# Slabs of two 64-slot units in a GRU with a top-2 mixture of experts, on one core

## The chip, the cores and the metric

One Trainium2 chip, one of its cores. The metric is device time in microseconds, the median of several executions. The engines are named as in the profile: PE (TensorE matmul), PEld (TensorE weight load), DVE (VectorE), ACT (ScalarE), POOL (GpSimd), SP (SyncE, which here issues nearly all DMAs). All data are float32.

## The reference

A GRU runs over `x` of shape (16, 256, 512): 16 sequences, 256 time steps, state size 512, started from `cond_2048`. Each of its 4096 output tokens then goes through a mixture of 8 experts, and the result is added to `x`.

```python
gi = x @ W_ih + b_ih;  gh = h @ W_hh + b_hh        # per time step
r = sigmoid(i_r + h_r); z = sigmoid(i_z + h_z)
n = tanh(i_n + r * h_n)
h_new = (1.0 - z) * n + z * h
...
router_logits = x / norm @ router_w                # x: the GRU's outputs, 4096 x 512
routing_weights = softmax(router_logits)
rw, selected_experts = top_k(routing_weights, 2);  rw = rw / sum(rw)
combine = sum(one_hot(selected_experts, 8) * rw[..., None], axis=1)
for e in range(8):
    out = out + combine[:, e, None] * (x @ Wa[e] @ Wb[e])   # Wa 512x128, Wb 128x512
...
x = x + out
```

## The kernel before

**The recurrence.** `step` (L910) emits one time step. The state lies as 128 partitions by 128 (four groups of 32, of which 16 rows are sequences), so that all matmuls use 32 columns of PE and four of them, one for each column group, run beside each other. PE multiplies the state with W_hh into the banks `rn` (L921) and `z` (L931). ACT forms `r` (L947) and `z` (L952), DVE `n` in two instructions (L954, L955), ACT its tanh (L956), and DVE `zh`, `m` and the new state `rows` (L959, L961, L963), which it transposes for PE (`hist`, L966). The next step's first matmul waits for that transpose. The part of W_ih (L269, L277) of the pair of steps to come is spread over the two steps before. Eight steps are a block of 128 tokens.

**The mixture.** Blocks 0 to 28 are dispatched, in four chunks of 7, 11, 7 and 4 blocks (`CHUNKS`). `Route` (L592) finds a block's two experts; its instructions on POOL are `nrm` (L629), a memset (L307) and `pre` (L637). When a chunk is complete, `Chunk` (L436) ranks its tokens, gives each expert a run of slots whose length is rounded up to 128, and POOL scatters the rows into slots in DRAM (L558, two indirect DMAs for each block). `Slab` (L648) then works on 128 slots of one expert. It loads the slots (`xg`, four DMAs of SP). POOL reads the expert's number into a register (L672) and copies the expert's Wa and Wb into `wag` and `wbg` (L677, L681). DVE transposes (`xgT`, L687). PE multiplies with Wa (L698; two halves, `down`) and with Wb (L713; two halves, `up`), ACT empties PSUM, and SP stores to DRAM. `Combine` (L737) gathers a block's two rows of each token back (L750, two indirect DMAs of POOL), and DVE adds them to `x` (L764). Blocks 29 to 31 are not dispatched: `Moe` (L778) runs all eight experts on them (L833, L854, L870).

A chunk of k blocks gets `(2 * 128 * k + 127 * 8) // 128` slabs, whatever the routing: 21, 29, 21 and 15, together 86.

**What sets the order.** All instructions are emitted in one order, and `keep_order` holds every engine to it. A planner places the mixture's work among the steps. Each agent's `plan` is a list of `Piece`s with a `gap` (steps since the piece before), a `cost` of PE time, and the buffers it `takes` and `gives` (counted in `ROOM`, L29). In each step `choose` (L1052) goes through the agents in order of rank; a piece with a cost is taken while the step's spare time (0.5, and 1.8 in the steps named by `EARLY`) is not used up, or against a credit that grows with the work left and the time to its deadline (L1060, L1073). After step 256 there is no recurrence left, and the rounds follow each other without it. A slab's plan before:

```python
Piece(then=[("load",)], takes="xg load", gives="load"),
Piece(gap=2, then=[("weights",)], takes="wg copy", gives="copy"),
Piece(gap=2, then=[("turn",)], takes="xt turn", gives="xg turn"),
Piece(cost=0.43, pe=[("down", 0)], takes="ps"),
Piece(gap=0, cost=0.43, pe=[("down", 1)], then=[("mid",)], takes="at", gives="ps xt"),
Piece(cost=0.43, pe=[("up", 0)], takes="ps"),
Piece(gap=0, cost=0.43, pe=[("up", 1)], then=[("store",)], gives="ps wg at"),
```

There are four buffers for the weights of slabs, so the copies for slab n+4 wait for the matmuls of slab n. The 12 `EARLY` pairs of steps had their W_ih part done long before, so their steps have 1.3 us of PE work less.

Of the kernel before, what the change touches and what calls it, by code (L numbers as in the profile page):

```python
# [8 lines left out]
FP = mybir.dt.float32  # L9
I32 = mybir.dt.int32  # L10
# [11 lines left out]
P = 128  # L22
TS = 8
CHUNKS = [7, 11, 7, 4]
LAG = 10
# [4 lines left out]
    "ps": 3, "xg": 4, "wg": 4, "xt": 2, "at": 2, "yg": 2, "xr": 3, "a": 1, "aT": 1,  # L30
    "hc": 1, "load": 2, "copy": 1, "turn": 2, "early": 2,
# [13 lines left out]
def gru_moe_kernel(  # L45
# [55 lines left out]
    HE = E // 2  # L101

# [43 lines left out]
    for side, src in enumerate((b_ih, b_hh)):  # L146
        for g in (0, 2, 1):
            tag = ("xg", "wbg")[side]
            b_rows[side, g] = slb.tile([1, D], FP, tag=tag, name=f"b_{side}_{g}")
            act.dma_start(b_rows[side, g], src[None, g * D : (g + 1) * D])  # L150
# [31 lines left out]
    SM = max((2 * P * k + (P - 1) * E) // P for k in CHUNKS)  # L182
    pages = const.tile([P, KM], FP, name="pages")
    for k in range(KM):
        pool.memset(pages[:, k : k + 1], float(P * k))
    count = const.tile([P, SM], FP, name="count")
    for k in range(SM):
        pool.memset(count[:, k : k + 1], float(k))
    before = const.tile([P, E, E], FP, name="before")
    pool.memset(before, 0.0)  # L190
    for e in range(1, E):
# [6 lines left out]
    n_slots = [  # L198
        max((2 * P * k + (P - 1) * E) // P for k in CHUNKS[n::2]) for n in range(2)
    ]  # L200
# [235 lines left out]
    class Chunk:  # L436


        def __init__(self, c, k):
            self.c, self.k = c, k  # L440
            self.n_slabs = (2 * P * k + (P - 1) * E) // P
# [30 lines left out]
        def places(self):  # L472
            c, k, S = self.c, self.k, self.n_slabs
            full = chk.tile([P, E, KM], FP, tag="full", name=f"full_{c}")
            dve.tensor_tensor(
                full[:, :, 0:k],
                self.rank[:, k, :, None].broadcast_to([P, E, k]),
                pages[:, None, 0:k].broadcast_to([P, E, k]),
                ALU.is_gt,
            )  # L480
            t8 = chk.tile([P, E], FP, tag="t8", name=f"t8_{c}")
            dve.reduce_sum(t8, full[:, :, 0:k], axis=AX.X)
            self.t8 = t8

        def places2(self):
# [10 lines left out]
                sv, first[:, None, :].broadcast_to([P, k, E]), float(P),  # L496
# [22 lines left out]
        def experts(self):  # L519
            c, k, S = self.c, self.k, self.n_slabs  # L520
            end = chk.tile([P, E], FP, tag="end", name=f"end_{c}")
            dve.tensor_add(end, self.first, self.t8)
            past = chk.tile([P, SM, E - 1], FP, tag="past", name=f"past_{c}")
# [6 lines left out]
            ef = chk.tile([P, SM], FP, tag="ef", name=f"ef_{c}")  # L530
            dve.reduce_sum(ef[:, 0:S], past[:, 0:S, :], axis=AX.X)
            self.expert = chk.tile([P, SM], I32, tag="expert", name=f"expert_{c}")
# [115 lines left out]
    class Slab:  # L648
# [21 lines left out]
        def weights(self):  # L670
            n = self.n
            e = pool.value_load(  # L672
                self.chunk.expert[0:1, n : n + 1], min_val=0, max_val=E - 1
            )
            self.wa = slb.tile([P, NQ, R], FP, tag="wag", name=f"wag_{self.name}")
            self.wb = slb.tile([P, D], FP, tag="wbg", name=f"wbg_{self.name}")
            pool.tensor_copy(  # L677
                self.wa,
                wa_sb[:, :, bass.ds(e, 1), :].rearrange("p q e r -> p (q e) r"),
            )  # L680
            pool.tensor_copy(  # L681
                self.wb, wb_sb[:, bass.ds(e, 1), :].rearrange("p e f -> p (e f)")
            )
# [8 lines left out]
        def down(self, n):  # L692
            if n == 0:
                self.ps = big(f"at_ps_{self.name}")
            for q in (2 * n, 2 * n + 1):
                for c in range(NJ):
                    c32 = slice(32 * c, 32 * c + 32)
                    pe.matmul(  # L698
                        self.ps[c32, 0:P], lhsT=self.wa[:, q, c32],
                        rhs=self.xt[:, q, :], start=(q == 0), stop=(q == NQ - 1),  # L700
# [6 lines left out]
        def up(self, n):  # L707
# [3 lines left out]
            for c in range(NJ):  # L711
                c32 = slice(32 * c, 32 * c + 32)
                pe.matmul(  # L713
                    self.ps[c32, half], lhsT=self.at[:, c32], rhs=self.wb[:, half],
# [9 lines left out]
        def plan(self):  # L724
            return [
                Piece(then=[("load",)], takes="xg load", gives="load"),
                Piece(gap=2, then=[("weights",)], takes="wg copy", gives="copy"),
                Piece(gap=2, then=[("turn",)], takes="xt turn", gives="xg turn"),
                Piece(cost=0.43, pe=[("down", 0)], takes="ps"),
                Piece(gap=0, cost=0.43, pe=[("down", 1)], then=[("mid",)],  # L730
                      takes="at", gives="ps xt"),
                Piece(cost=0.43, pe=[("up", 0)], takes="ps"),
                Piece(gap=0, cost=0.43, pe=[("up", 1)], then=[("store",)],
                      gives="ps wg at"),
# [43 lines left out]
    class Moe:  # L778
# [4 lines left out]
        def prep(self):  # L783
# [7 lines left out]
            self.sq = moe.tile([P, NQ, P], FP, tag="a", bufs=1, name=f"sq_{i}")  # L791
# [28 lines left out]
        def soft3(self):  # L820
# [4 lines left out]
            self.a = moe.tile([P, E, R], FP, tag="a", bufs=1, name=f"a_{i}")  # L825
            self.aT = moe.tile([P, E, P], FP, tag="aT", bufs=1, name=f"aT_{i}")
# [16 lines left out]
        def scale(self, s):  # L843
            e4 = slice(s * HE, (s + 1) * HE)
            dve.tensor_mul(
                self.a[:, e4, :],
# [4 lines left out]
        def trans(self, s):  # L851
            ps = big(f"aT_ps_{self.i}_{s}")
            for k in range(HE):
                pe.transpose(  # L854
                    ps[:, k * P : (k + 1) * P], self.a[:, s * HE + k, :], ident
                )
            self.ps["t", s] = ps

        def evict(self, s):
            act.copy(  # L860
                self.aT[:, s * HE : (s + 1) * HE, :].rearrange("p e t -> p (e t)"),
# [3 lines left out]
        def up(self, e):  # L865
            if e == 0:
                self.ps["o"] = big(f"o_ps_{self.i}")
            for c in range(NJ):
# [3 lines left out]
                    lhsT=self.aT[:, e, c32],  # L872
# [138 lines left out]
    n_slabs = [(2 * P * k + (P - 1) * E) // P for k in CHUNKS]  # L1011
# [186 lines left out]
```

## Time and profile before

| | |
|---|---|
| time, median of 6 executions | 1302.6 us (1300.65 to 1305.58) |
| the profiled execution's own time | 1303.33 us |
| its span, first to last instruction | 1301.6 us |
| busy PE / PEld / DVE / ACT / POOL | 1254.1 / 896.0 / 737.7 / 391.3 / 285.4 us |
| mean granted PE clock | 0.99 |
| POOL copies `wag` (L677) | 86, 661 ns mean |
| POOL copies `wbg` (L681) | 86, 649 ns mean |
| first `hist` transpose ends (step 1) | 36.7 us |
| last `hist` transpose ends (step 256) | 1219.2 us |

How to read it: "busy" is the time in which an engine has an instruction under way, and a line such as "L677 POOL COPY wag<-wa_sb 128x512 f32 x86" is a group of 86 instructions of line 677 which write `wag` from `wa_sb`. In a timeline the columns are the start and the duration in us, engine, line, operation, output and input, shape and count; in brackets, the idle time of the engine ahead of it and what ended that. A matmul of float32 shows as two instructions, each with its own weight load.

The time falls into three parts: 36.7 us until the first step is done, 1182.5 us for the other 255 steps, and 82.4 us after the last one.

### The profile page before, as it was taken

How to read it: one execution, taken by the hardware profiler on the slowest of the kernel's cores; microseconds unless marked ns; L12 is line 12 of the kernel's file. 1: busy time of each engine (PE TensorE's matmuls, PEld its weight loads, DVE VectorE, ACT ScalarE, POOL GpSimd, SP SyncE). 2: the span in 40 equal slices, each digit the busy share in tenths (PEclk: the TensorE clock that was granted, in tenths of full speed). 3: DMA queues.
4: the chain of work that ended last, by engine and by line, in shares of the span. 5: the costliest groups of instructions: out<-in, count | busy, mean ns of one | idle time of the engine just before them, and what ended most of it. 6: DMA issues, size and time to landing. Idle time of an engine off the chain costs nothing. (4 is left out here: it accounts for less than half of the span.)

```text
span 1301.6 us, 68450 instructions
## 1 busy us (share of the span) xinstructions
PE 1254.1 (96%) x30378; PEld 896.0 (69%) x30378; DVE 737.7 (57%) x2678; ACT 391.3 (30%) x1354; POOL 285.4 (22%) x504
## 2 busy tenths in 40 slices
PE   7899999999999999999999989999999999999986
PEld 3577777777677777777776756777777778777642
DVE  1455555556565555555656636666566466776643
ACT  1232222222232333333333323333333323333220
POOL 2000000002321100000102313232114234273542
PEclk7999999999999999999999989999999999999999
DMA  8532322222422212111112644654336456674786
GB/s 209 146 128 70 134 79 84 99 67 82 154 79 67 61 49 55 57 47 56 56 44 76 194 142 117 177 154 142 97 95 204 134 151 172 192 229 141 214 243 179
DMA packets 149477, 158.67 MB, mean 122 GB/s; under 512 B 22646, under 2 KB 103606, under 8 KB 149180
## 3 DMA queue, kind: packets, MB, share of 16 engines
q1 hardware_dynamic: 139760, 123.83, 32.3%
q0 software_dynamic: 9280, 30.42, 7.6%
q8 instruction: 238, 3.90, 1.3%
q14 instruction: 59, 0.48, 0.1%
q10 hardware_dynamic: 140, 0.05, 0.0%
HBM read 84.21 MB, written 69.99 MB: 118 GB/s over the span
## 5 line engine op out<-in xcount | busy, mean ns | idle before, releaser
L921 PE MATMUL rn<-whh,hist 128*32 128x256 f32 x8160 | 495.4, 382 | 16.9 <-DVE hist L966 14.0
L921 PEld LDWEIGHTS rn<-whh,hist 128*32 128x32 f32 x8160 | 251.1, 110 | 196.5 <-DVE hist L966 48.8
L269 PE MATMUL rn<-wih,xT 128*32 128x256 f32 x3712 | 291.5, 383 | 13.6 <-DMA wih<-in_L_cond_W_ih_dram 7.9
L954 DVE SCALAR_TENSOR_TENSOR n<-r,rn 128x128 f32<-128x128 f32 x256 | 73.4, 287 | 367.9 <-ACT r L947 367.7
L931 PE MATMUL z<-whh,hist 128*32 128x128 f32 x8160 | 272.5, 273 | 0.0
L931 PEld LDWEIGHTS z<-whh,hist 128*32 128x32 f32 x8160 | 236.6, 110 | 41.9 <-issue 0.2
L947 ACT ACTIVATE r<-rn 128x128 f32<-128x128 f32 x256 | 71.1, 278 | 427.6 <-PE rn L921 426.7
L277 PE MATMUL z<-wih,xT 128*32 128x128 f32 x3712 | 192.5, 275 | 0.0
L277 PEld LDWEIGHTS z<-wih,xT 128*32 128x32 f32 x3712 | 124.6, 111 | 79.3 <-issue 2.7
L269 PEld LDWEIGHTS rn<-wih,xT 128*32 128x32 f32 x3712 | 115.3, 111 | 15.5 <-ACT rn L249 6.3
L952 ACT ACTIVATE z<-z 128x128 f32<-128x128 f32 x256 | 71.1, 278 | 150.5 <-PE z L931 150.5
L959 DVE SCALAR_TENSOR_TENSOR zh<-z,h 128x128 f32<-128x128 f32 x255 | 77.8, 305 | 65.3 <-ACT z L952 64.7
L629 POOL TENSOR_TENSOR nrm<-ss,half 128x1 f32<-128x1 f32 x29 | 16.3, 561 | 405.9 <-ACT ht L627 385.9
L698 PE MATMUL at_ps<-xgT,wag 128*32 128x128 f32 x2752 | 98.6, 274 | 3.3 <-POOL nrm L815 1.7
L713 PE MATMUL y_ps<-wbg,at 128*32 128x256 f32 x1376 | 96.2, 380 | 0.1
L698 PEld LDWEIGHTS at_ps<-xgT,wag 128*32 128x32 f32 x2752 | 81.0, 111 | 10.1 <-issue 3.5
L966 DVE STREAM_TRANSPOSE hist<-rows 128x128 f32<-128x128 f32 x256 | 79.8, 312 | 8.7
L974 DVE STREAM_TRANSPOSE h<-hist 128x128 f32<-128x128 f32 x256 | 79.7, 311 | 8.7
L963 DVE SCALAR_TENSOR_TENSOR rows<-zh,m 128x128 f32<-128x128 f32 x256 | 76.9, 301 | 8.9
L681 POOL COPY wbg<-wb_sb 128x512 f32 x86 | 55.8, 649 | 115.3 <-PE y_ps L713 115.3
L721 ACT COPY y<-y_ps 128x512 f32<-128x512 f32 x86 | 50.2, 584 | 97.6 <-PE y_ps L713 86.0
L956 ACT ACTIVATE n<-n 128x128 f32<-128x128 f32 x256 | 77.2, 302 | 4.8 <-DVE n L955 4.5
(136 smaller groups left out, 1056.3 us busy)
## 6 DMA issues: line engine op xcount, KB each, us to landing
xg<-x_slots SPq DMA_DIRECT2D x344, 64.0 KB
y_slots<-y SPq DMA_DIRECT2D x86, 256.0 KB
ht<-H SPq DMA_DIRECT2D x58, 256.0 KB
x_slots<-zero SPq DMA_DIRECT2D x50, 256.0 KB
x<-in_x_dram SPq DMA_DIRECT2D x256, 32.0 KB
xr<-in_x_dram SPq DMA_DIRECT2D x32, 256.0 KB
out_dram<-xr SPq DMA_DIRECT2D x32, 256.0 KB
H<-rows SPq DMA_DIRECT2D x232, 32.0 KB
```

The lines of the kernel that those rows point to most:

```text
L269: pe.matmul(rn[32 * j : 32 * j + 32, 0 : 3 * P].rearrange("p (g d) -> p g d", g=3)[:, 0:3:2, :], lhsT=xts[m][:, q, :], rhs=w[:, 0:3:2, j, ...
L277: ins = pe.matmul(zb[32 * j : 32 * j + 32, 0:P], lhsT=xts[m][:, q, :], rhs=w[:, 1, j, :], start=False, stop=(q == NQ - 1), skip_group_chec ...
L698: pe.matmul(self.ps[c32, 0:P], lhsT=self.wa[:, q, c32], rhs=self.xt[:, q, :], start=(q == 0), stop=(q == NQ - 1),)
L713: pe.matmul(self.ps[c32, half], lhsT=self.at[:, c32], rhs=self.wb[:, half], start=True, stop=True,)
L921: pe.matmul(rn[32 * j : 32 * j + 32, 0 : 2 * P].rearrange("p (g d) -> p g d", g=2), lhsT=hT[:, q, :], rhs=w(q, j)[:, 0:3:2, :], start=Fals ...
L931: pe.matmul(zb[32 * j : 32 * j + 32, 0:P], lhsT=hT[:, q, :], rhs=w(q, j)[:, 1, :], start=False, stop=(q == NQ - 1), skip_group_check=True,)
L954: dve.scalar_tensor_tensor(n, r, 1.0, rn[:, P : 2 * P], ALU.add, ALU.mult)
L956: act.activation(n, n, AF.Tanh)
L959: dve.scalar_tensor_tensor(zh, z, 1.0, hrow, ALU.add, ALU.mult)
L963: dve.scalar_tensor_tensor(hn, zh, 0.5, m, ALU.mult, ALU.subtract)
L966: dve.transpose(hist[:, t, :, lo : lo + 32], hn.rearrange("p (q c) -> p q c", q=NQ))
L974: dve.transpose(hrow.rearrange("p (q c) -> p q c", q=NQ), hT)
```

## The change

A slab's 128 slots become two units of 64 (`U = 64`), and each unit may belong to another expert. The runs of an expert are rounded up to 64 slots instead of 128. A chunk has `(2 * 128 * k + 63 * 8) // 64` units and half as many slabs, rounded up: 18, 26, 18 and 12, together 74. `down(u)` now works on one unit with all of the contraction instead of on all 128 slots with half of it: 16 matmul calls of 64 columns for each unit, before 8 of 128 for each half. `up` has the same calls, and takes the Wb of the unit to which the 32 output rows belong. POOL copies Wa and Wb for both units, with a register read ahead of each copy, in two pieces of the plan (`weights_a`, `weights_b`); the weight buffers are twice as large, and three instead of four.

The tables `pages` and `count` are longer (22 and 52 memsets at the start, before 11 and 29), and the small DVE instructions of `Chunk` that use them are wider. To make room, the dense blocks' `sq`, `a` and `aT` use the tags `ht` and `ht2` of the dispatched rows, in halves. Fewer slabs also mean fewer slots to clear at the start.

```diff
+U = 64
-    "ps": 3, "xg": 4, "wg": 4, "xt": 2, "at": 2, "yg": 2, "xr": 3, "a": 1, "aT": 1,
-    "hc": 1, "load": 2, "copy": 1, "turn": 2, "early": 2,
+    "ps": 3, "xg": 4, "wa": 3, "wb": 3, "xt": 2, "at": 2, "yg": 2, "xr": 3, "a": 1, "aT": 1,
+    "hc": 1, "load": 2, "copy": 2, "turn": 2, "early": 2,
...
+    NU = P // U
+    def n_units(k):
+        return (2 * P * k + (U - 1) * E) // U
+    def slabs_of(k):
+        return (n_units(k) + NU - 1) // NU
...
-    for k in range(KM):
-        pool.memset(pages[:, k : k + 1], float(P * k))
+    for k in range(NU * KM):
+        pool.memset(pages[:, k : k + 1], float(U * k))
...
-        def weights(self):
-            n = self.n
-            e = pool.value_load(
-                self.chunk.expert[0:1, n : n + 1], min_val=0, max_val=E - 1
-            )
-            self.wa = slb.tile([P, NQ, R], FP, tag="wag", name=f"wag_{self.name}")
-            self.wb = slb.tile([P, D], FP, tag="wbg", name=f"wbg_{self.name}")
...
+        def expert(self, u):
+            k = NU * self.n + u
+            return pool.value_load(
+                self.chunk.expert[0:1, k : k + 1], min_val=0, max_val=E - 1
+            )
+        def weights_a(self):
+            self.wa = slb.tile(
+                [P, NU, NQ, R], FP, tag="wag", bufs=3, name=f"wag_{self.name}"
+            )
+            for u in range(NU):
+                e = self.expert(u)
+                pool.tensor_copy(
+                    self.wa[:, u, :, :],
+                    wa_sb[:, :, bass.ds(e, 1), :].rearrange("p q e r -> p (q e) r"),
+                )
+        def weights_b(self):
+            self.wb = slb.tile([P, NU, D], FP, tag="wbg", bufs=3, name=f"wbg_{self.name}")
+            for u in range(NU):
+                e = self.expert(u)
+                pool.tensor_copy(
+                    self.wb[:, u, :],
+                    wb_sb[:, bass.ds(e, 1), :].rearrange("p e f -> p (e f)"),
+                )
...
-        def down(self, n):
-            if n == 0:
+        def down(self, u):
+            if u == 0:
                 self.ps = big(f"at_ps_{self.name}")
-            for q in (2 * n, 2 * n + 1):
+            us = slice(U * u, U * u + U)
+            for q in range(NQ):
                 for c in range(NJ):
                     c32 = slice(32 * c, 32 * c + 32)
                     pe.matmul(
-                        self.ps[c32, 0:P], lhsT=self.wa[:, q, c32],
-                        rhs=self.xt[:, q, :], start=(q == 0), stop=(q == NQ - 1),
+                        self.ps[c32, us], lhsT=self.wa[:, u, q, c32],
+                        rhs=self.xt[:, q, us], start=(q == 0), stop=(q == NQ - 1),
                     )
...
-                    self.ps[c32, half], lhsT=self.at[:, c32], rhs=self.wb[:, half],
+                    self.ps[c32, half], lhsT=self.at[:, c32],
+                    rhs=self.wb[:, 32 * c // U, half],
...
-                Piece(gap=2, then=[("weights",)], takes="wg copy", gives="copy"),
-                Piece(gap=2, then=[("turn",)], takes="xt turn", gives="xg turn"),
-                Piece(cost=0.43, pe=[("down", 0)], takes="ps"),
-                Piece(gap=0, cost=0.43, pe=[("down", 1)], then=[("mid",)],
-                      takes="at", gives="ps xt"),
+                Piece(gap=2, then=[("weights_a",)], takes="wa copy", gives="copy"),
+                Piece(then=[("weights_b",)], takes="wb copy", gives="copy"),
+                Piece(then=[("turn",)], takes="xt turn", gives="xg turn"),
+                Piece(cost=0.45, pe=[("down", 0)], takes="ps"),
+                Piece(gap=0, cost=0.45, pe=[("down", 1)], then=[("mid",)],
+                      takes="at", gives="ps xt wa"),
                 Piece(cost=0.43, pe=[("up", 0)], takes="ps"),
                 Piece(gap=0, cost=0.43, pe=[("up", 1)], then=[("store",)],
-                      gives="ps wg at"),
+                      gives="ps wb at"),
...
-            self.sq = moe.tile([P, NQ, P], FP, tag="a", bufs=1, name=f"sq_{i}")
+            self.sq = moe.tile([P, NQ, P], FP, tag="ht", name=f"sq_{i}")
...
-            self.a = moe.tile([P, E, R], FP, tag="a", bufs=1, name=f"a_{i}")
-            self.aT = moe.tile([P, E, P], FP, tag="aT", bufs=1, name=f"aT_{i}")
+            self.a, self.aT = {}, {}
...
+            self.a[s] = moe.tile([P, HE, R], FP, tag="ht", name=f"a_{self.i}_{s}")
...
+            self.aT[s] = moe.tile([P, HE, P], FP, tag="ht2", name=f"aT_{self.i}_{s}")
```

## The prediction

> **What bounds the kernel now.** I read the groups first, then the stretches, then timelines of single steps. Busy shares mislead here: PE is busy 96% of the span, yet much of that is work that fits into a step for nothing. So I took the ends of the 256 `hist` transposes (L966) as a clock of the recurrence. 165 of the 255 gaps between them are 4.40 us, whether a slab's half lies in the step or not: there the chain PE, ACT, DVE sets the pace, with room for one piece of some 0.43 us on PE. The other gaps sum to 59.5 us over 4.40 each. Two kinds of excess can be told apart.
>
> In the first, PE holds more than one piece: the next step's first matmul starts 0.44 us late for a second piece, 0.87 for a third. In the second PE is on time and DVE is late, as in this step of 4.82 us (485.93 to 490.75):
>
> ```profile
> 487.67 0.20 POOL L637 TENSOR_TENSOR pre<-pre,mask 128x8 f32<-128x8 f32 x1 [10.26 <-DVE mask L318]
> ...
> 488.61 0.29 DVE L955 SCALAR_TENSOR_TENSOR n<-n,rn 128x128 f32<-128x128 f32 x1
> 488.63 0.61 POOL L677 COPY wag<-wa_sb 128x512 f32 x1 [0.76 <-PE rn L921]
> ...
> 489.17 0.29 DVE L959 SCALAR_TENSOR_TENSOR zh<-z,h 128x128 f32<-128x128 f32 x1 [0.27 <-ACT z L952]
> 489.18 0.76 POOL L681 COPY wbg<-wb_sb 128x512 f32 x1
> 489.26 0.61 PE L269 MATMUL rn<-wih,xT 128*32 128x256 f32 x8
> 489.38 0.70 DVE L961 SCALAR_TENSOR_TENSOR m<-z,n 128x128 f32<-128x128 f32 x1
> ```
>
> `m` takes 0.70 us beside a POOL copy; its median over 256 is 0.284. L955, which has one operand in PSUM, keeps its 0.29 beside a copy. So a copy that meets `zh`, `m` or `rows` (two operands in SBUF each) holds the chain up, by 0.41 us for one and up to 0.93 when copies follow each other under all three. Summed over the lengthened `zh`, `m` and `rows` of the trace this is 10.5 us, 3 of it around 1141 us, where the dense block's preparation joins in. The copy in this step came at that moment because POOL's order puts it behind `pre`, which waits for DVE.
>
> The stretches (duration, then busy PE, PEld, DVE, ACT, POOL) show chunk 1's slabs, chunk 2's, and the end:
>
> ```profile
> 798.70:1046.60 247.90, 242.31 (x6132) 180.04 (x6132) 154.62 (x550) 87.00 (x294) 65.31 (x102) 1.00 0.49 143
> 1046.60:1168.40 121.80, 118.87 (x3047) 94.00 (x3051) 84.39 (x273) 40.68 (x134) 56.41 (x75) 1.00 0.65 188
> ...
> 1219.20:1301.60 82.40, 67.61 (x1077) 35.22 (x1068) 35.74 (x75) 14.44 (x35) 37.68 (x51) 0.96 0.75 220
> ```
>
> In the last, no step is left and PE is busy 67.6 of 82.4 us: there PE work removed is time removed, as long as POOL, at 37.7 us, keeps up.
>
> **A slab on PE.** These lines give the pace (PE instructions in groups of four, one for each column group):
>
> ```profile
> 902.70 1.06 PE L698 MATMUL at_ps<-xgT,wag 128*32 128x128 f32 x32
> ...
> 1244.99 0.47 PE L803 MATMUL rt<-sq,ones 128*1 128x32 f32 x32
> ...
> 1251.53 0.84 PEld L698 LDWEIGHTS at_ps<-xgT,wag 128*32 128x32 f32 x32 [2.17 <-POOL nrm L815]
> 1251.56 1.08 PE L698 MATMUL at_ps<-xgT,wag 128*32 128x128 f32 x32 [1.72 <-POOL nrm L815]
> ```
>
> 32 instructions of 128 columns are 8 groups; less the 0.27 of the last and 0.02 for its stagger, 7 intervals of 0.109 us. So `down` costs 0.87 us, and `up`, 4 groups of 256 columns at 0.216, 0.865. After the change `down` is 16 groups of 64 columns. By columns that is 16 x 0.055 = 0.88. The loads could bound it instead. The last fence shows a matmul starting 0.03 us after its load, below 0.055, and in its second line 32 matmuls of 32 columns (0.19 us each) take 0.47 us, 0.009 from start to start, 0.036 a group. I take 0.055, nearest to these rows; the bounds are 0.036 (0.58 a slab, 0.3 less than before) and 0.109, should each group wait for loads as now (1.74 a slab, 0.87 more). A slab so stays at 1.74, and the 12 fewer save 20.9 us of PE work.
>
> The Trainium skill speaks against this: "TensorE: Matmul & The Clock Gate", section "Wait — 56ns, not 53.3ns?", says that matmuls never start closer than about 25 ns. By it `down` would have 64 x 0.025 = 1.6 us, 0.7 us a slab more, an estimate of 53 us of PE work over 74 slabs. The row of L803 differs, 0.009 from start to start with four column groups, and I go by the row.
>
> **Where the saving lands.** I worked `choose` through step by step with both plans; for the old one it gives the pieces that the trace shows in each step. That yields an order, no time. With 0.45 us free in a normal step, 1.75 in an early one, and the durations above, PE's overhang in steps 2 to 256 falls from 40.9 to 30.9 us: 10.0 saved. Chunk 0's slabs mostly fitted for nothing; chunk 1 gives 5.9, chunk 2 2.5. PE work left after step 256 falls from 66.1 to 57.6, 8.5 saved. There slabs also fill dense blocks' waits (scale, transpose, eviction), two or three times some 0.7 us; I give back 2: 6.5 saved.
>
> **The copies.** A slab has four copies of 0.61 us, before two: 296 instead of 172. Each has its own register read (0.29, then 0.15 and some 0.2 of POOL's queue), so a run of copies goes at about 0.72 us each, an estimate from these rows. Walking POOL's order through (copies wait for the matmuls of three slabs before, for `nrm` at the end of a step, for `pre` 1.7 us into one) gives 154 copies and 16 struck steps before, 272 and 34 after, up to step 256; the trace has some 20, most of them the steps that the walk names. In ten of the 34 a run of about eight copies starts behind `nrm`, at a step's beginning, and lies under all three instructions. I price these at 0.8 (0.71, 0.87 and 0.93 in the trace), fourteen single ones at 0.45, the rest with the dense preparation at 5: 19.3. Less 10.5 before, +9. Bounds: 0 extra, if the runs end ahead of `zh`; +18, if all 34 steps lose some 0.84 (28.5 us).
>
> POOL is also late for others. In step 215 DVE waits 1.1 us for POOL's memset behind scatters; the walk makes that 1.8 longer and about 0.2 elsewhere: +2, from 0 to 6. After step 256 POOL has 18 us of copies, 13 of gathers and preparation in the 30 us up to dense block 30's transposes, where PE has 29. It just keeps up; a late `nrm` can cost 1.5 us, within the 2 given back.
>
> **At nothing.** The 34 more memsets (0.035 us from one to the next) lie ahead of W_ih's arrival at 10.8 us, and step 1 waits for W_hh until after 30; uncovered they would cost 1.2 us. The wider `Chunk` instructions (0.37 us for 203 elements, some 0.2 more for 364) stand on DVE while it waits for `r`, 0.37 us or less if not. SP issues 60 DMAs for slabs and 6 clears fewer; the 11 us step at 762.40 waits for rows stored and read back (`ht` at L627, 7.98 us), in a queue which the change leaves as it is, so I leave it; it could go by some us either way. The shared tags order `sq`, `a` and `aT` behind readers that the planner's `hc` and `a` already kept apart; uncovered, a dense block's transposes, 0.7 us.
>
> **The sum**, on the profiled execution of 1303.33 (span 1301.6, 1.7 around it): -10.0 - 6.5 + 9 + 2 = -5.5. It lies 0.7 above the median of 1302.6, so 1297.1; I say 1297.
>
> **The rivals.** 0.2% (2.6 us) is about what a measurement here can tell from no change: 1300.0 to 1305.2 counts as the same.
>
> - Forecast, 1292 to 1300: chance 0.33.
> - The runs of copies fall while DVE waits for `r`, and only PE's saving is left: -16.5, 1286. For it speaks that `zh` starts only 3.2 us into a step of 4.4; against it, that a run of eight lasts 5.6 us. Chance 0.17.
> - The terms cancel: 1302. Chance 0.15.
> - Slower: POOL's copies become the chain's brake in chunks 1 and 2. With the upper bounds, +18 + 6 - 16.5 = +7.5, 1310. It decides from the point where collisions and lateness add over 16.5 us, so 27 us in all. For it: 56.4 of 121.8 us POOL is busy already in chunk 2, and its order is fixed. Against it: over half of the copies before start in the first 1.75 us of a step, when DVE has none of the three. Chance 0.25.
> - Slower: weight loads pace the short matmuls, 0.87 us a slab on PE, 64 over 74 slabs; as one piece fits a step and would be twice as long, nearly all shows: +64 + 11 - 16.5, some 1360. Chance 0.10.
>
> Faster 0.50, same 0.15, slower 0.35. The range is 1284 to 1313: it leaves out the last rival and the rims. The likeliest case's own range is 1292 to 1300.
>
> **What would show it.** Right: a unit's 32 matmul instructions on `at_ps` in about 0.6 us; the last `hist` at 1217 to 1222; the stretch after it 74 to 77 us; lengthened `m` in about 30 steps. Wrong: those 32 in 1.0 us or more; or `hist` gaps over 5.3 in most of chunks 1 and 2; or PE waiting for `wag` in the steps.

## The result and the profile after

The changed kernel takes 1308.96 us (median of 20 executions, 1303.35 to 1316.55), the kernel before 1302.59 (42 executions): 1.0052 of it, 95% interval 1.0039 to 1.0064. That is slower by 0.5%, where the forecast was 1297. The profiled execution has a span of 1306.6 us against 1301.6.

The groups of the slabs in the page of the changed kernel (busy time, mean of one in ns, then the idle time ahead), and the queue that brings TensorE's instructions:

```profile
q8 instruction: 252, 4.13, 1.4%
...
L986 DVE SCALAR_TENSOR_TENSOR zh<-z,h 128x128 f32<-128x128 f32 x255 | 85.4, 335 | 64.3 <-ACT z L979 63.7
...
L703 POOL COPY wbg<-wb_sb 128x512 f32 x148 | 94.7, 650 | 91.5 <-PE y_ps L737 77.9
L694 POOL COPY wag<-wa_sb 128x512 f32 x148 | 93.5, 639 | 89.0 <-PE at_ps L722 70.5
...
L722 PE MATMUL at_ps<-xgT,wag 128*32 128x64 f32 x4736 | 87.4, 219 | 4.1 <-issue 3.9
```

The slabs' work is what was foreseen: 4736 matmuls of 64 columns, whose groups of four follow each other after 0.056 us in the median run of 32, and 296 copies. The stretches of chunks 1 and 2 and the end, with the columns as in the prediction's table:

```profile
804.00:1054.90 250.90, 239.64 (x6836) 179.83 (x6832) 156.16 (x542) 84.21 (x288) 89.50 (x142) 1.00 0.42 124
1054.90:1177.60 122.70, 117.43 (x3444) 96.23 (x3436) 86.59 (x273) 40.66 (x134) 72.36 (x102) 1.00 0.61 178
1230.03:1306.56 76.53, 62.58 (x1152) 30.48 (x1144) 32.27 (x71) 11.64 (x27) 42.79 (x58) 0.94 0.72 211
```

In both chunks PE is busy for less time than before and POOL for 16 to 24 us more, yet the stretches are 3.0 and 0.9 us longer. The end is 5.8 us shorter.

**Where the time went.** Each step can be cut at four events, counted from the `hist` end of the step before: the start of its first `rn` matmul (0.055 us when nothing is late), the start of `r` on ACT (2.005 later), of the first `n` on DVE (0.31 later), and its own `hist` end (2.04 later). What each part has above these numbers, summed over steps 2 to 256, with the start and the end (one profiled execution of each kernel, differences taken before rounding):

| us | before | after | difference | forecast |
|---|---|---|---|---|
| end of step 1 | 36.7 | 39.2 | +2.5 | 0 |
| first `rn` matmul late (PE's overhang) | 35.1 | 28.2 | -6.9 | -10.0 |
| `rn` matmuls themselves | 9.4 | 8.9 | -0.5 | 0 |
| first `n` late (DVE is held up ahead of it) | 4.5 | 10.0 | +5.6 | +2 |
| `zh`, `m`, `rows` lengthened | 10.5 | 21.3 | +10.8 | +9 |
| the rest of that part | -1.5 | -2.2 | -0.7 | 0 |
| after step 256 | 82.3 | 76.5 | -5.8 | -6.5 |
| span | 1301.6 | 1306.6 | +5.0 | -5.5 |

No term has the wrong sign, and most miss by 1 to 4 us in the same direction. The changed kernel's executions spread over 13 us, so a single profile fixes no term to a microsecond. The two largest lengthenings are longer than any in the profile before. Step 245 (DVE and POOL; lines of other engines left out):

```profile
1170.76 1.18 POOL L703 COPY wbg<-wb_sb 128x512 f32 x2
...
1171.62 3.23 DVE L986 SCALAR_TENSOR_TENSOR zh<-z,h 128x128 f32<-128x128 f32 x1 [0.27 <-ACT z L979]
1171.87 1.17 POOL L694 COPY wag<-wa_sb 128x512 f32 x2
1172.98 1.16 POOL L703 COPY wbg<-wb_sb 128x512 f32 x2
...
1174.09 1.22 POOL L694 COPY wag<-wa_sb 128x512 f32 x2
...
1174.77 0.69 DVE L988 SCALAR_TENSOR_TENSOR m<-z,n 128x128 f32<-128x128 f32 x1
```

One `zh` takes 3.23 us: it starts inside a run of copies, and the copies behind the first, each following the last without a pause, pass ahead of it, five in all. Step 168 has another of 2.13 us. The prediction priced a run of copies at 0.8, by steps that lost up to 0.93; these two lost 3.3 and 2.6 with their `m` and `rows`. The profile before had the same thing once in small, in a step that the prediction put down to the dense block's preparation:

```profile
1141.73 0.70 POOL L681 COPY wbg<-wb_sb 128x512 f32 x1
...
1142.00 1.64 DVE L963 SCALAR_TENSOR_TENSOR rows<-zh,m 128x128 f32<-128x128 f32 x1
...
1142.38 1.51 POOL L787 COPY hc<-hist 128x128 f32<-128x128 f32 x4
```

There `rows` starts inside a copy, and three of the four short copies behind it pass ahead.

The late first `n` is the other cost of POOL's order. Step 215:

```profile
1017.28 0.26 DVE L320 TENSOR_SCALAR pr<-ex,rs 128x8 f32<-128x8 f32 x1
1017.33 0.98 POOL L569 DMA_INDIRECT x_slots<-ht,ihi  x1 [0.21 <-issue]
...
1018.62 0.97 POOL L569 DMA_INDIRECT x_slots<-ht,ilo  x1 [0.30 <-issue]
...
1019.58 0.12 POOL L317 MEMSET pr<- 128x6 f32 x1
1019.74 0.18 DVE L322 MAX8 m<-pr 128x8 f32<-128x14 f32 x1 [2.21 <-POOL pr L317]
```

DVE waits 2.21 us for a memset of 0.12 that stands behind two scatters, which a copy (it ends at 1017.12) had made late. In the whole profile DVE waits 7.5 us in five places for this memset, before 2.1 in two; 6.8 and 1.3 of it lie in the steps.

PE's overhang fell by less than foreseen because PE at times had nothing to execute ("issue": no wait that the profile shows). Step 172, PE alone:

```profile
808.80 1.19 PE L722 MATMUL at_ps<-xgT,wag 128*32 128x64 f32 x72
811.10 0.32 PE L722 MATMUL at_ps<-xgT,wag 128*32 128x64 f32 x8 [1.11 <-issue]
```

The queue `q8` brings PE's instructions in packets of 16 KB (4.13 MB over 252). In the trace a packet starts at 808.21, PE runs dry at 809.8 after some 200 more instructions, and resumes at 811.10, 2.9 us after the packet's start. In step 211 the same happens from 993.37 to 996.63, 3.3 us. The transfers of these two packets took 1.5 and 1.9 us. PE has six more such waits in the steps, at `at_ps` (steps 236, 244, 245) and `z`, and all eight end 2.3 to 3.3 us after a packet's start, as does the one in the profile before. That PE waits for the instructions in these packets is read from this regularity; the profile names no releaser. A step's own matmuls use 200 instructions in about 5 us; the short ones use them in 1.4. PE's waits of this kind, outside step 165 and the `rn` of the state, are 6.3 us at `at_ps` (3.9) and `z` (2.4), all in the steps; before there is one of 1.3 us, and it lies behind step 256.

### The profile page after: what moved, and what is told of

Read it like the earlier page. It is cut to its first block, busy times and chain, and to the rows that moved or that the text cites. A ratio compares the mean times of both kernels' runs of the same rounds, so it can differ in the third digit from the quotient of the medians.

```text
span 1306.6 us, 72777 instructions
## 1 busy us (share of the span) xinstructions
PE 1244.1 (95%) x32170; PEld 893.8 (68%) x32170; DVE 742.5 (57%) x2666; ACT 383.0 (29%) x1330; POOL 366.2 (28%) x662
## 3 DMA queue, kind: packets, MB, share of 16 engines
q8 instruction: 252, 4.13, 1.4%
## 4 chain that ended last, share of the span: by engine, by line
PE 79%; DMA 9%; DVE 5%; SPq 2%; issue 2%; ACT 1%; POOL 1%; POOLq 0%; ACTq 0%; DVEq 0%
PE rn L948 33%; PE z L958 16%; PE rn L279 12%; PE z L287 6%; PE at_ps L722 4%; PE y_ps L737 4%; DMA xr<-in_x_dram 2%; PE gi L387 1%; DMA ht<-H 1%; DMA whh<-in_L_cond_W_hh_dram 1%; DVE zh L986 1%; DVE rows L990 1%; PE rt L351 1%; DMA wih<-in_L_cond_W_ih_dram 1%; DVE hist L993 1%
## 5 line engine op out<-in xcount | busy, mean ns | idle before, releaser
L986 DVE SCALAR_TENSOR_TENSOR zh<-z,h 128x128 f32<-128x128 f32 x255 | 85.4, 335 | 64.3 <-ACT z L979 63.7
L703 POOL COPY wbg<-wb_sb 128x512 f32 x148 | 94.7, 650 | 91.5 <-PE y_ps L737 77.9
L694 POOL COPY wag<-wa_sb 128x512 f32 x148 | 93.5, 639 | 89.0 <-PE at_ps L722 70.5
L722 PE MATMUL at_ps<-xgT,wag 128*32 128x64 f32 x4736 | 87.4, 219 | 4.1 <-issue 3.9
L737 PE MATMUL y_ps<-wbg,at 128*32 128x256 f32 x1184 | 84.7, 382 | 0.5 <-ACT at L729 0.5
L990 DVE SCALAR_TENSOR_TENSOR rows<-zh,m 128x128 f32<-128x128 f32 x256 | 79.5, 310 | 8.9
```

The costliest lines, as they stand in the source:

```text
L694: pool.tensor_copy(self.wa[:, u, :, :], wa_sb[:, :, bass.ds(e, 1), :].rearrange("p q e r -> p (q e) r"),)
L703: pool.tensor_copy(self.wb[:, u, :], wb_sb[:, bass.ds(e, 1), :].rearrange("p e f -> p (e f)"),)
L722: pe.matmul(self.ps[c32, us], lhsT=self.wa[:, u, q, c32], rhs=self.xt[:, q, us], start=(q == 0), stop=(q == NQ - 1),)
L737: pe.matmul(self.ps[c32, half], lhsT=self.at[:, c32], rhs=self.wb[:, 32 * c // U, half], start=True, stop=True,)
L986: dve.scalar_tensor_tensor(zh, z, 1.0, hrow, ALU.add, ALU.mult)
L990: dve.scalar_tensor_tensor(hn, zh, 0.5, m, ALU.mult, ALU.subtract)
```

## The experiments

They ran on four chips, on which the kernel before takes 1358 to 1363 us, not 1303. So each run is held against the kernel before on its own chip, and sizes don't carry over one to one. What differs is seen in the last section.

**e1 to e4: the copies taken away, and their collisions taken away.** e1 and e2 leave out every weight copy of the kernel before and of the changed one; the dispatched rows get wrong weights.

```diff
-                        self.ps[c32, us], lhsT=self.wa[:, u, q, c32],
+                        self.ps[c32, us], lhsT=wa_sb[:, q, u, c32],
...
-                    rhs=self.wb[:, 32 * c // U, half],
+                    rhs=wb_sb[:, 32 * c // U, half],
```

> The kernel before, its 172 weight copies on GpSimd left out (the slabs' matmuls read one fixed expert's weights where they lie, so the dispatched rows get wrong weights); every matmul, its order and its shape stay. Theory (GpSimd's copies hold up the chain's VectorE instructions): the 10.5 us of lengthening in 19 steps go, and perhaps 2 to 4 us of lateness of what queues behind them: 1288 to 1292 us. Rival (TensorE's work alone sets the time and the copies are hidden): within 2 us of 1302.6.

> The changed kernel, its 296 weight copies left out in the same way (two fixed experts, one for each unit: wrong weights for the dispatched rows). Theory: the change's saving on TensorE is whole (-10.0 in steps 2 to 256, -6 behind them) and what it lost lies in the second copies: this kernel is 10 to 16 us faster than the kernel before without copies, about 1274 to 1282 us, and some 27 to 35 us faster than the changed kernel. Rival (the 64-column matmuls, the new order of pieces or the shared buffers cost what was lost, not the copies): 4 to 8 us slower than the kernel before without copies, about 1294 to 1298 us.

Measured: 0.9980 of the kernel before (0.9966 to 0.9993) and 0.9976 (0.9963 to 0.9988). Lengthening falls to 1.1 and 0.3 us. Neither theory held: without any copies the changed kernel should have been 10 to 16 us faster than the one before, and the two are alike. So the copies were not all that the change lost by; something on PE eats the saving of twelve slabs. (What takes the saving is tried in e6 and e13 to e15.)

e3 and e4 keep every copy and put one operand of each of the three DVE instructions into PSUM:

```diff
-        z = new("z", 4)
+        z = zb[:, (1 + t % 2) * P : (2 + t % 2) * P]
...
-        m = new("m", 2)
+        m = rn[:, 3 * P : 4 * P]
```

> The kernel before; the step's z (written by ScalarE) and m (written by VectorE) lie in unused columns of the step's two PSUM banks, so that each of zh, m and rows has one operand that is not in SBUF; the copies stay. Theory (a VectorE instruction waits for a GpSimd copy when both its operands lie in SBUF, as zh, m and rows have them, and n1 and n2, with one operand in PSUM, never lengthened): the 10.5 us go, 1290 to 1294 us. Rival (the lengthening has another cause, such as the copies' traffic as such): 1302 us or, with slower access to PSUM, up to 1310.

> The changed kernel with z and m in PSUM in the same way; all 296 copies stay, and nothing is left out. Theory: the 21.3 us of lengthening go, lateness of GpSimd's other work stays: 1286 to 1291 us, that is faster than the kernel before with z and m in PSUM by 1 to 7 us. Rival (the lengthening has another cause): 1309 us or above.

Measured: 0.9956 (0.9939 to 0.9974) and 0.9955 (0.9936 to 0.9973), both some 6 us below the kernel before, where e4 was expected 1 to 7 us below e3. **e8** is e4 once more, beside **e7**, the changed kernel once more:

> The changed kernel once more, nothing altered, beside the others on one chip. Theory: 0.4 to 0.7 per cent above the kernel before, the first step's end again within 1 us of the kernel before's own spread. Rival (the 34 more memsets at the start cost 2.5 us): the first step ends at 39 us here and at 37 us in the two kernels of this call that are built from the one before.

> The changed kernel with z and m in PSUM, once more, since the chip of its first run was some 4 per cent slower with every kernel, the one before too. Theory: zh, m and rows are never lengthened, and it is 11 to 20 us below the kernel before on a chip where that takes 1303. Rival (what was lost is not the lengthening): at or above the kernel before.

e7: 1.0024 (1.0010 to 1.0038), so on these chips the change costs half of what it did in the pair, less than the 0.4 to 0.7% expected. e8: 0.9945 (0.9930 to 0.9961), so 0.79% or 10.7 us below e7. That e8 would be 11 to 20 us below the kernel before can't be judged here, since e7 shows 10.6 us of lengthening and not 21.3. But the size agrees with what e7 has to lose. The DVE groups of e7, then of e8:

```profile
L986 DVE SCALAR_TENSOR_TENSOR zh<-z,h 128x128 f32<-128x128 f32 x255 | 79.5, 312 | 100.8 <-ACT z L979 99.9 <-issue 0.5
L990 DVE SCALAR_TENSOR_TENSOR rows<-zh,m 128x128 f32<-128x128 f32 x256 | 77.8, 304 | 8.9
```

```profile
L986 DVE SCALAR_TENSOR_TENSOR zh<-z,h 128x128 f32<-128x128 f32 x255 | 74.4, 292 | 98.8 <-ACT z L979 95.3 <-issue 2.9
L990 DVE SCALAR_TENSOR_TENSOR rows<-zh,rn 128x128 f32<-128x128 f32 x256 | 73.5, 287 | 8.8
```

With an operand in PSUM (`m` lies in the bank `rn` there) not one of the 768 instructions takes over 0.300 us, in e3, e4 and e8 alike, beside the same copies. The instructions themselves don't gain by it: in the median `m` takes 0.300 us instead of 0.284, `zh` 0.292 and `rows` 0.287 instead of 0.292. This settles which instructions the copies hold up. One thing doesn't fit: without any copies e1 and e2 gain less (0.20%, and 0.48% from e7) than e3 and e8 do with them (0.44% and 0.79%), though both ways end the lengthening. The intervals of e1 and e3 overlap a little; why the two ways differ is open; with 128-column downs the two ways are worth the same (e14, e15 below). The Trainium skill, "SBUF — State Buffer", section "SBUF: two separate sides", has the rule: a VectorE instruction with two SBUF inputs and a GpSimd instruction that reads SBUF exclude each other for the whole instruction. The trace agrees on who collides. The page speaks of the instruction that holds the ports; that a waiting one stays out through five copies in a row, so that it takes 3.23 us, is only in the trace.

**e5: the copies doubled, nothing else.** The kernel before, each copy made twice:

```diff
+            for _ in range(2):
-            pool.tensor_copy(
-                self.wa,
+                pool.tensor_copy(
+                    self.wa,
...
```

> The kernel before; each of the 172 weight copies is made twice, the second one over the first, back to back on GpSimd (344 copies; the changed kernel has 296). Everything else stays, TensorE's work and the buffers too. Theory (the second copies are what the change lost by): zh, m and rows lengthen in some 36 steps instead of 19, 21 us or more instead of 10.5, and work queued behind the copies comes late: 8 to 18 us slower than the kernel before on the same chip. Rival (copies are hidden, the loss is in TensorE's short matmuls or the shared buffers): within 3 us of the kernel before.

Measured: 1.0127 (1.0111 to 1.0142), +17 us. The lengthening is 29.2 us, against 8.0 in the kernel before on such a chip (e9). In e5:

```profile
L960 DVE SCALAR_TENSOR_TENSOR zh<-z,h 128x128 f32<-128x128 f32 x255 | 86.4, 339 | 99.8 <-ACT z L953 97.8 <-issue 1.7
L964 DVE SCALAR_TENSOR_TENSOR rows<-zh,m 128x128 f32<-128x128 f32 x256 | 82.6, 322 | 8.9
L962 DVE SCALAR_TENSOR_TENSOR m<-z,n 128x128 f32<-128x128 f32 x256 | 82.5, 322 | 1.6 <-ACT n L957 1.0
```

As the theory had it: copies on an engine that is busy 22% of the span (28% in e5) cost time because they lengthen the chain, here by 21 us more for 17 us of time. Six `zh` here take 1.08 to 1.83 us, each passed by one or more copies.

**e6: the short matmuls alone.** The kernel before, `down` in halves of 64 slots with the same weights:

```diff
-            for q in (2 * n, 2 * n + 1):
+            us = slice(64 * n, 64 * n + 64)
+            for q in range(NQ):
...
-                        self.ps[c32, 0:P], lhsT=self.wa[:, q, c32],
-                        rhs=self.xt[:, q, :], start=(q == 0), stop=(q == NQ - 1),
+                        self.ps[c32, us], lhsT=self.wa[:, q, c32],
+                        rhs=self.xt[:, q, us], start=(q == 0), stop=(q == NQ - 1),
```

> The kernel before; only the down product of each slab is issued in halves of 64 slots, as in the changed kernel: 32 matmuls of 64 columns instead of 16 of 128, with the same weights. Theory (a group of four costs half as much, 0.055 us against 0.109): within 2 us of the kernel before. Rival (each short matmul is held up by its weight load or by a fixed cost): the 86 slabs take up to 0.7 us more each, and as the slabs lie behind the steps' own work, 10 to 55 us slower.

Measured: 1.0126 (1.0105 to 1.0147), +17 us, where my theory said within 2. The rival's price was right and its mechanism not: runs of 32 instructions still go at 0.056 us for a group of four. What grew are waits without a cause that the profile shows.

**e9 to e11: a profile of the kernel before on such a chip; the memsets; the shared buffers.**

```diff
+    extra = const.tile([P, 34], FP, name="extra")
+    for k in range(34):
+        pool.memset(extra[:, k : k + 1], float(k))
```

> The kernel before, nothing altered, with a profile from a chip of the experiments: it is what the profiles of the other runs are to be held against. Theory: ratio 1.000; lengthening of zh, m and rows 7 to 11 us; gaps in TensorE's work (other than those in which it waits for the step's own state) 45 to 53 us in steps 2 to 256, as in the other kernels with 128-column downs, and lower than the 58 to 66 us of the kernels with 64-column downs.

> The kernel before with 34 more one-column memsets on GpSimd at the start, as many as the changed kernel adds there. Theory (the first step's later end, 39.2 against 36.7 us, is a difference between executions): ratio 1.000, the first step ends within 0.5 us of the kernel before on this chip. Rival (the memsets delay what TensorE needs first): 1.2 to 2.5 us slower, all of it before the first step's end.

> The kernel before with the dense blocks' buffers shared with dispatched rows as in the changed kernel, and nothing else of the change. Theory (the sharing costs no step anything): within 1.5 us of the kernel before. Rival (sharing makes a dense block wait for a dispatched row's fetch, or the other way round): 2 to 6 us slower, in the steps after 222 and behind step 256.

e11's edit is the part of the change that touches `sq`, `a`, `aT`, `full` and `past`. Measured: e9 0.9997 (0.9986 to 1.0009), lengthening 8.0 us, and some 50 us of gaps in PE's work in steps 2 to 256 (time between the starts of two matmuls that the first one's columns don't account for, without the waits for the state), against 58 to 66 in the kernels with 64-column downs (e2, e4, e6, e7, e8). e10 1.0010 (0.9997 to 1.0022), its first step ends at 38.5 us, e9's at 38.6: the memsets cost the start nothing. e11 1.0002 (0.9990 to 1.0015): nor does the sharing cost anything. The 2.5 us by which the changed kernel's first step ended later lie in the load of W_hh: DVE's last scaling of it (L994, L1021 after) starts at 32.95 us before and at 35.46 after. Why the load is late stays unexplained. In the experiments the first step ends between 38.4 and 40.0 us, at 38.7 in the mean of the eight built from the kernel before and at 39.4 in that of the ten built from the changed one, so some 0.6 us may belong to the change.

**e12: the late memset on DVE**, on top of e8: `dve.memset(pr[:, E:14], 2.0)` for `pool.memset`.

> The changed kernel with z and m in PSUM, and the small memset that pads the router's probabilities (GpSimd's, behind the scatters, 7.5 us of waits of VectorE in the changed kernel's profile, 2.1 before) made by VectorE. Nothing is left out. Theory: below the changed kernel with z and m in PSUM alone (0.9945 to 0.9955 of the kernel before) by a further 3 to 5 us: 0.991 to 0.993. Rival (those waits are covered by TensorE's work): no lower than 0.9945.

Measured: 0.9954 (0.9939 to 0.9969), no gain over e8. It tests nothing, since in e7's profile DVE no longer waits for that memset at all: with longer steps POOL gets there in time. Whether it would save the 7.5 us of the profiled pair was not found out.

**e13 to e15: the changed kernel with half the instructions in `down`.** All 128 slots with the first unit's weights, so that a second unit of another expert gets wrong ones; copies, plan and `up` stay. e14 drops the copies as well, e15 has `z` and `m` in PSUM.

```diff
-            us = slice(U * u, U * u + U)
-            for q in range(NQ):
+            for q in (2 * u, 2 * u + 1):
...
-                        self.ps[c32, us], lhsT=self.wa[:, u, q, c32],
-                        rhs=self.xt[:, q, us], start=(q == 0), stop=(q == NQ - 1),
+                        self.ps[c32, 0:P], lhsT=self.wa[:, 0, q, c32],
+                        rhs=self.xt[:, q, :], start=(q == 0), stop=(q == NQ - 1),
```

> The changed kernel; only the down product of a slab is issued over all 128 slots with the first unit's weights (half as many TensorE instructions in it; the second unit's rows get wrong weights where its expert is another). All 296 copies, the buffers, the plan and the up product stay. Theory (the short matmuls cost nothing in their own rate, but TensorE runs out of instructions in them): 10 to 15 us faster than the changed kernel on these chips, that is 0.991 to 0.995 of the kernel before, with gaps in TensorE's work back at 45 to 53 us in steps 2 to 256. Rival (the 64-column downs cost nothing): as the changed kernel, 1.001 to 1.004, gaps still 58 to 66 us.

> The changed kernel with 128-column downs as in the run before this one, and without any weight copy (one fixed expert, two in the up product: wrong weights for the dispatched rows). Theory: the whole saving of 74 slabs for 86 is left, 12 to 17 us against the kernel before without copies (0.998): 0.985 to 0.989. Rival (fewer slabs save little on these chips, because the slabs fill time in which TensorE would wait anyway): above 0.993.

> The changed kernel with 128-column downs and with z and m in PSUM; all copies stay (the second unit's rows get the first unit's weights in the down product). Theory: the saving of e13 and that of z and m in PSUM add up: 0.982 to 0.988. Rival (they are the same time counted twice): no lower than 0.991.

Measured: e13 0.9968 (0.9951 to 0.9984), 0.56% or 7.6 us below e7, less than I expected but well beyond the rival; e14 0.9886 (0.9864 to 0.9907), as expected, 12 us below e2, and 13 us below e1; e15 0.9887 (0.9866 to 0.9907), a little above what was expected. These sums go across chips, each by its ratio to the kernel before. So twelve slabs fewer are worth 13 us, the short downs take 8 to 12 of them, and the copies' collisions 11: the two costs add up (0.56 + 0.79 against 1.37% for both). PE's waits for `at_ps` without a visible cause, in e9 (before), e6, e7 (the changed kernel) and e13:

```profile
PE at_ps L698 <- issue: 4.5, 14, 0.4
```

```profile
PE at_ps L699 <- issue: 9.0, 19, 1.6
```

```profile
PE at_ps L722 <- issue: 13.2, 26, 1.6
```

```profile
PE at_ps L721 <- issue: 3.9, 12, 0.5
```

Twice the instructions, 9.0 and 13.2 us; half of them, 4.5 and 3.9. That is 4.5 and 9.3 us of the 17 and 7.6; the rest is not traced to single waits. And on these chips the waits lie beside POOL's indirect DMAs: all of them in e9, e6 and e13, and 10.5 of the 13.2 in e7, begin within 4 us of the start of one. Of the pair's 3.9 us only 1.0 do. So these runs show that 64-column downs cost time, but not that they cost it in the pair by the same way. Gaps in PE's work in the steps fell only from 59 to 56 us in e13, not to the 45 to 53 of my expectation; the rest of its gain lies behind step 256 (74.7 us against 79.5).

**e16 to e18: fewer instructions in `up`.** e16 gives the changed kernel with `z` and `m` in PSUM an `up` in matmuls of 512 columns, two column groups to a piece. e17 and e18 issue all four groups in one piece, in the changed kernel and in the one before:

```diff
             if n == 0:
                 self.ps = big(f"y_ps_{self.name}")
+                return
...
-                    self.ps[c32, half], lhsT=self.at[:, c32], rhs=self.wb[:, half],
+                    self.ps[c32, :], lhsT=self.at[:, c32], rhs=self.wb,
```

> The changed kernel with z and m in PSUM, and the up product issued in matmuls of 512 columns, half as many as of 256. Nothing is left out. Theory (instructions of TensorE are what is short): 2 to 5 us below the changed kernel with z and m in PSUM (0.9945 to 0.9955), 0.991 to 0.994. Rival (only instructions in short matmuls cost anything): 0.994 to 0.996.

> The changed kernel with z and m in PSUM, and the up product in one set of four matmuls of 512 columns, one for each column group, in the place of two sets of 256 columns (e16 put two groups side by side instead of four, and so took twice the time on TensorE). Nothing is left out. Theory (TensorE runs out of instructions in the slabs): 2 to 6 us below the changed kernel with z and m in PSUM, 0.990 to 0.994. Rival (only the 64-column downs use instructions faster than they come): 0.994 to 0.996.

> The kernel before with z and m in PSUM and the same up product in one set. Nothing is left out. Theory: 1 to 5 us below the kernel before with z and m in PSUM (0.9956), 0.992 to 0.995, and no faster than the same version of the changed kernel. Rival: 0.995 to 0.997.

Measured: e16 1.0029 (1.0011 to 1.0047), e17 1.0009 (0.9994 to 1.0024), e18 1.0008 (0.9993 to 1.0024): all worse than e8 and e3 by 0.5% or more, outside both theories. e16 was badly made: in its trace two groups of 512 columns take 0.43 us and the next two 0.43 more, where four groups of 256 take 0.215, so `up` costs twice the time. In e17 and e18 all of `up`, 0.87 us, falls into one step, and the first `rn` matmul is late by 48.1 and 43.7 us in sum, against 41.6 and 40.0 in e8 and e3. That these larger pieces overflow the steps is the likely reason; it wasn't tried apart. So fewer instructions are no gain in themselves; the shortage shows in the 64-column matmuls.

**The best version.** `z` and `m` in PSUM: 0.9945 and 0.9955 with the change (e8, e4), 0.9956 without (e3). On these chips both beat both kernels; which is better can't be told from these runs.

## Why the prediction was wrong, step by step

- **The bound** (the chain sets the pace, a copy beside `zh`, `m` or `rows` holds it up): right, and shown by e3, e4, e5 and e8.
- **A slab on PE, "I take 0.055":** right for the rate (0.056; a unit's 32 instructions in 0.62 to 0.72 us where nothing interrupts them), so the weight loads' rival at 1360 falls. The floor of some 25 ns that the Trainium skill gives ("TensorE: Matmul & The Clock Gate", "Wait — 56ns, not 53.3ns?") doesn't hold here either: 7 ns from one of a group's matmuls to the next. But a rate is what PE does while it has instructions. That a denser stream can outrun their supply was not among the terms. A sign of it was in the profile before: PE waited 1.3 us at `at_ps` on "issue", once, behind step 256.
- **Where the saving lands, -10.0:** this term failed by 3.1 us (-6.9). The 3.9 us of PE's "issue" waits at `at_ps`, in steps 172, 211, 236, 244 and 245, are of the size that it lacks, and in each of these steps the first `rn` matmul is late, by 0.5 to 2.2 us. Of the waits at `z` 1.8 us lie in step 245, hidden behind the `zh` shown above. That this is the cause is read from the trace. e6 and e13 to e15 show that short downs cost time, 8 to 17 us on their chips, mostly beside indirect DMAs there. The levels of the working were off as well: it had 40.9 and 30.9 us of overhang, and the profiles show 35.1 and 28.2.
- **After step 256, -6.5:** right (-5.8; the stretch is 76.5, in the 74 to 77 named). The last `hist` came at 1230.0, not at 1217 to 1222.
- **The copies, +9:** nearly right in sum (+10.8) and in steps (36 struck against 34), partly by chance: two steps alone hold 5.9 of the 21.3 us, through waits longer than any that I priced, while most others cost less than the 0.8 I gave to runs. `m` lengthened in 14 steps, not 30; `zh` takes the brunt, in 28.
- **POOL late for others, +2 (0 to 6):** the mechanism right, the size near its upper bound: +5.6, some 4.2 of it DVE waiting for the memset behind scatters. In step 215 that wait was 1.3 us before (not 1.1) and 2.2 after, but steps 159 and 167 added 2.5 and 0.7 that the walk did not have. No run tests it, since e12 met none of these waits.
- **At nothing:** the shared buffers and the memsets are free (e11, e10). The first step's 2.5 us, in the load of W_hh, were not among the terms, and their cause stays open.

What decides the sign: collisions (21.3) and lateness (10.0) came to 31.4 us. The 27 from which the rival at 1310 was to decide held the collisions before, 10.5, but not the 4.5 of lateness; with it the point is 31.5. They grew by 16.4, as much as the 16.5 that PE was to save, so by themselves they would have brought the time back to that before. PE saved 12.7 (6.9 + 5.8), and the start added 2.5, other parts of the steps -1.2: 16.4 - 12.7 + 2.5 - 1.2 = +5.0. So the steps that failed are three terms: PE's saving in the steps (-10.0, measured -6.9), POOL's lateness (+2, measured +5.6) and the start (0, measured +2.5); the copies (+9, measured +10.8) add less. It went that rival's way, with one term near its upper bound, and with PE's saving and the start off in the same direction, which no rival had. I had put the terms of one engine's order at or near the middle of their bounds while they share a cause: more copies make everything on POOL late at once.

## What to carry to other kernels

Before a copy is given to an idle engine, look at which of the chain's instructions have both operands in SBUF: a run of copies can keep one of them waiting through several, and an operand in PSUM ends it. When matmuls are made shorter, count instructions per microsecond as well as columns, and look for "issue" waits on PE. And when several small costs come from one queue, they can grow together; here both of POOL's came out above the middle of their bounds.

## What the runs showed of the hardware that was not expected

- **A waiting DVE instruction doesn't get in between copies that follow each other at once:** `zh` took 2.13 and 3.23 us in the changed kernel instead of 0.29, `rows` 1.64 in the kernel before.
- **PE can run out of instructions**, as far as the trace tells. Its eight waits without a visible cause in the steps end 2.3 to 3.3 us after the start of a packet of instructions. The Trainium skill, "Runtime: NRT & Kernel Launch", section "Instruction fetch mechanics", calls the fetch of 16 KB blocks mostly hidden; the blocks agree (16 KB each), but in these bursts the fetch seems not to be hidden.
- **On the chips of the experiments PE slows down beside indirect DMAs.** In e9 47 of the some 50 us of gaps in PE's steps begin within 4 us of the start of one of the 116 scatters and gathers, a fifth of the time; in the profile of the kernel before 2 of 13, not counting one wait of 5.9 us at 765 us, which ACT ends. The first chunk's scatters in e9, POOL and then PE:

```profile
317.75 1.21 POOL L558 DMA_INDIRECT x_slots<-ht,ihi  x1 [8.23 <-DVE ilo L514]
319.26 0.99 POOL L558 DMA_INDIRECT x_slots<-ht,ilo  x1 [0.31 <-issue]
320.55 0.98 POOL L558 DMA_INDIRECT x_slots<-ht,ihi  x1 [0.30 <-issue]
```

```profile
320.57 0.42 PE L277 MATMUL z<-wih,xT 128*32 128x128 f32 x5
321.32 0.30 PE L277 MATMUL z<-wih,xT 128*32 128x128 f32 x2 [0.33 <-issue]
321.35 0.40 PE L269 MATMUL rn<-wih,xT 128*32 128x256 f32 x1
321.46 0.27 PE L277 MATMUL z<-wih,xT 128*32 128x128 f32 x1
321.58 1.61 PE L269 MATMUL rn<-wih,xT 128*32 128x256 f32 x7
323.94 0.43 PE L277 MATMUL z<-wih,xT 128*32 128x128 f32 x8 [0.74 <-ACT z L952]
```

The profile of the kernel before has the same matmuls beside the same scatters:

```profile
318.24 0.61 PE L269 MATMUL rn<-wih,xT 128*32 128x256 f32 x8
318.67 0.40 PE L277 MATMUL z<-wih,xT 128*32 128x128 f32 x8
```

The eight of `rn`, 0.61 us there, are strewn from 321.35 to 323.19 in e9. The two profiles' spans differ by 63 us; the gaps in PE's work by 38, and the steps' part "`rn` matmuls themselves" by 31 (40.1 against 9.4). What sets these chips apart, and whether the shortage of instructions in e6 and e13 is the same effect at work, stays open.
